# Context attention: output projections in 64x128 tiles over four PSUM banks, and context values of both batches in one go

## The chip, the cores and the metric

The kernel runs on one core of a Trainium2 chip. The metric is device time in microseconds, the median of several runs. Matrix products run on TensorE (PE in the profile; PEld is its weight loads), element-wise work on VectorE (DVE), ScalarE (ACT) and GpSimd (POOL), and most transfers are issued by SyncE (SP). Matrix products write to PSUM, which has eight banks of 128 partitions by 512 fp32 values.

## The reference

All data are fp32. Two batches of 1024 tokens with 256 features go through a transformer block: self attention, attention to a context of 154 tokens with 192 features, and a gated feed-forward layer, each behind a layer norm and with a residual. There are 16 heads of 64.

```python
def _attention(xq, xkv, wq, wk, wv, wo, bo):
    q = (xq @ wq).reshape(B, S, N_HEADS, D_HEAD)
    k = (xkv @ wk).reshape(B, T, N_HEADS, D_HEAD)
    v = (xkv @ wv).reshape(B, T, N_HEADS, D_HEAD)
    attn = softmax(einsum('bihd,bjhd->bhij', q, k) * D_HEAD ** -0.5)
    out = einsum('bhij,bjhd->bihd', attn, v).reshape(B, S, D_ATTN)
    return out @ wo + bo

h = _layernorm(x, ln1_g, ln1_b)
x = _attention(h, h, sa_wq, sa_wk, sa_wv, sa_wo, sa_bo) + x
h = _layernorm(x, ln2_g, ln2_b)
x = _attention(h, cond_emb, ca_wq, ca_wk, ca_wv, ca_wo, ca_bo) + x
h = _layernorm(x, ln3_g, ln3_b)
p = h @ ff_w1 + ff_b1
a, gate = p[..., :D_FF], p[..., D_FF:]
x = (a * gelu(gate)) @ ff_w2 + ff_b2 + x
```

## The kernel before

**Units and steps.** The 16 heads are taken as 8 pairs, so that each attention has 16 units: unit `ui` is batch `ui // 8`, head pair `ui % 8`. The program is one stream written out by hand (`tc.manual_schedule`): each engine runs its instructions in the order in which the code issues them. Self attention is the loop over `p` (8 steps a unit), context attention the loop over `c` (3 steps a unit, `ui, n = divmod(c, 3)`: three, three and two of a batch's eight token tiles of 128). The feed-forward layer follows.

**A step of context attention.** `cross_first(c)` issues the scores on TensorE (L999, tile `sc`) and the maxima on DVE (L1004). Then the copies that earlier products left in `stores` are issued, and `then` issues the exponentials on ACT (L1017, three or two for each of two heads). A function passed to `then` as `between` is issued between the two heads' exponentials. In the next step POOL divides by the sums (L1028), and two steps on DVE transposes the weights in 32x32 blocks (`cross_drain`, L1044). What else a step does depends on `n`:

- First step (`n == 0`): `cross_values(ui - 2)` multiplies the weights of the unit before last with its values (L1064, tile `poc`), in 32x64 tiles over four banks, the two `mm` and the two `sum` banks. DVE and ACT copy them out (L1075).
- Second step (`n == 1`): `cross_queries` makes the next unit's queries (L411, tile `pq_ca`) in 64x128 tiles on the two `mm` banks. ACT copies them out (L426) in the third step, behind the second step's exponentials and ahead of the third's.
- Third step (`n == 2`): an output piece (`out_piece`, L523, tile `py_ca` or `py_sa`), in even units the context values of one batch for two head pairs (`context_values`, L961, tile `pv_ca`), a norm's transposes where one is due (L323, tile `ph_ln`), and another output piece.

Units 1 and 15 also run output pieces in their second step: two each. Unit 1 runs one in its third step, and the fourth of that group runs in unit 2.

**Banks.** `mm_tile` and `sum_tile` each go round two banks (L70, L73); scores have the other four. A bank can be written again when the engine that read it last is done.

**Output pieces.** `out_piece` multiplies two token tiles with the output weights of two head pairs in 128x128 tiles: four `matmul` calls into one bank. An fp32 `matmul` stands as two rows in the trace, so a piece is eight rows. DVE adds a piece to `x` in one instruction of 512 columns (L530). A group of two head pairs has four pieces a batch; `cross_beside` queues a group at the first step of each odd unit from 3 on.

**Rounds.** Self attention's groups go through `out_rounds` (L536) instead: four token tiles at a time in 64x32 tiles, over the two `sum` banks (first pair of tiles) and the two `mm` banks (second pair). Both 64-row halves of TensorE work at once on the two banks of a pair; then they swap banks. `cross(pair, 0)` of both pairs is issued at once; before each pair's swapped half, a one-element copy by ACT (`seen`, L556) reads the bank and so separates the halves. Four adds of 256 columns follow on DVE (L562).

**Context values.** `context_values(b, pr)` multiplies a batch's first 128 context tokens with the value weights of two head pairs: 192 features in two 96-row matmuls, four rows. ACT copies the result (L968), SP writes it to DRAM (L969) and reads it back four times in another layout (L973). The last context tokens of all heads come from `context_ends`, whose result lies in `ends` until it has been sent to DRAM. Unit 0's values are made in self attention's step `SA - 2`, together with the keys of the last two head pairs (`context_keys`, L898, tile `pk`).

**Norms.** `norm_beside` queues a norm's statistics, normalisation and transposes in `side`; `run_work` takes one of them a step, and transposes only in a third step with an `mm` bank. The second batch's norm ahead of context attention is queued in unit 2 (its transposes run in units 3 to 6), the first batch's norm ahead of the feed-forward layer in unit 11 (transposes in units 12 to 15); their statistics (L266) run on DVE.

**SP's queue.** `load_ahead` issues self attention's loads and moves after each step's exchange of maxima and sums between partitions (L610).

Of the kernel before, what the change touches and what calls it, by code (L numbers as in the profile page):

```python
# [8 lines left out]
F32 = mybir.dt.float32  # L9
# [4 lines left out]
P = 128  # L14
# [4 lines left out]
def tile_transformer_block(ctx: ExitStack, tc: tile.TileContext, a: dict, out: bass.AP):  # L19
    nc = tc.nc  # L20
# [9 lines left out]
    NQ = 4  # L30
# [116 lines left out]
    def load_weights(kind, pr, what):  # L147
# [3 lines left out]
        elif kind == "sa" or what == "q":  # L151
            wsl[kind, pr, what] = load_slice(f"{kind}_w{what}", pr * P, P, HR)
        elif pr % 2 == 0:
            wsl[kind, pr, what] = load_slice(f"{kind}_w{what}", pr * P, VC, CC)
# [381 lines left out]
    def out_rounds(b, g, tiles):  # L536

        o = oT["sa", b, g]
        py = [bank(f"pr{b}_{g}_{t}") for bank, t in zip([sum_tile] * 2 + [mm_tile] * 2, tiles)]

        def cross(pair, swapped):
            for i in range(HP):
                for f in range(0, P, KB):
                    for r in (1, 0):
# [3 lines left out]
                            py[at][f:f + KB, :D], lhsT=o[own, i, t0:t0 + KB],  # L548
                            rhs=wo["sa", b, g][own, i, :],
# [9 lines left out]
        def add(at):  # L559
# [3 lines left out]
            added.add(("sa", b, g, t))  # L563

        for pair in range(2):
            cross(pair, 0)
        return [lambda pair=pair: second(pair) for pair in range(2)], [
            lambda at=at: add(at) for at in range(4)]

# [239 lines left out]
    held, kept, rounds = [], [], []  # L809

    def self_beside(ui):
# [15 lines left out]
        if ui >= HP and ui % HP == 0:  # L827
            ob, og = divmod(ui // HP - 1, NQ)
            for t0 in range(0, NG * 2, 2):
                rounds.append(  # L830
                    (ob, og, [t + e for t in out_order("sa")[t0:t0 + 2] for e in range(2)]))
# [3 lines left out]
    coming, ahead_ends = [], []  # L835
    to_dram = [(1, 3), (1, 6), (3, 3)]
    from_dram = [(NU - 1, n) for n in (0, 3, 5)]

    def load_ahead(p):
# [17 lines left out]
        if ahead_ends and (ui == 1 and n == SH + 1 or ui == 2 and n in (0, 1, SH)):  # L857
            ahead_ends.pop(0)()
        if (ui, n) in to_dram:
# [94 lines left out]
    def context_values(b, pr, bank=mm_tile):  # L954
# [3 lines left out]
        v = vs["ca", b, pr // 2] = pt_.tile([P, NB, VC], F32, tag="V", name=f"v_ca{b}_{pr}")  # L958
        pv = bank(f"pv_ca{b}_{pr}")
        for c in range(2):  # L960
            nc.tensor.matmul(  # L961
                pv[:, :VC], lhsT=ctxT[:, c, b * TP:b * TP + P],
                rhs=wsl["ca", pr, "v"][:, c, :], start=(c == 0), stop=(c == 1),
            )

        def store():
            own = one.tile([P, VC], F32, tag="own_v", name=f"own_v{b}_{pr}")
            nc.scalar.copy(own, pv[:, :VC])  # L968
            later.insert(0, lambda: nc.sync.dma_start(out=vd[b, pr][:P, :], in_=own))  # L969

            def back(a0):
                for a4 in range(a0, a0 + 2):
                    nc.sync.dma_start(  # L973
                        out=v[a4 * KB:(a4 + 1) * KB, :, :],
                        in_=vd[b, pr].rearrange("(n p) d -> p n d", p=KB))

# [620 lines left out]
```

## Time and profile before

| | |
|---|---|
| median of 3 runs | 1060.45 us (1059.89 to 1060.54) |
| the profiled execution | 1060.44 us, its span 1058.6 us |
| granted TensorE clock | 1.00 |
| busy: PE, PEld, DVE, ACT, POOL | 1047.1, 740.3, 880.7, 658.9, 769.9 us |
| context attention's scores | first at 687.57 us, last at 886.73 us |

Busy time is a share of the whole span. A row of a timeline gives start, length, engine, line, tile, tile shape on TensorE (rows x columns of the array) and how many instructions are merged; in brackets stands idle time before it and what ended it. The length of a merged TensorE line reaches to the end of its last matmul, which overlaps the next line's first, so that differences of starts tell what a group takes.

### The profile page before, as it was taken

Reading aid. Unit: us, or ns where it says so; the run is one execution under the profiler, and the core shown is the slowest. Engines: PE = TensorE matmul, PEld = TensorE weight load, DVE = VectorE, ACT = ScalarE, POOL = GpSimd, SP = SyncE. Lnnn points to the kernel's source line nnn. Section 1 sums busy time; section 2 is a strip of 40 time slices with the busy share of each in tenths; the row PEclk is TensorE's granted clock in tenths of the full one; section 3 lists DMA queues with packets and bytes.
Section 4 is the critical chain, followed back from the end, with each engine's and each line's share of the span. In section 5 each row is a group of like instructions: output and inputs, shape, how many; then the busy total and the mean of one; then the engine's idle time right before and its main releaser. Section 6 shows DMA issues by size and latency. Waiting matters only on the chain.

```text
span 1058.6 us, 51303 instructions
## 1 busy us (share of the span) xinstructions
PE 1047.1 (99%) x21700; PEld 740.3 (70%) x21700; DVE 880.7 (83%) x1313; ACT 658.9 (62%) x2147; POOL 769.9 (73%) x1620
## 2 busy tenths in 40 slices
PE   8999999999999999999999999999999999999998
PEld 6456965556576666665786676666676667889997
DVE  5799999999899999999999999968776777675654
ACT  5776767777776766766776777666666655243221
POOL 2677777788778777777777777757665777598773
PEclk9999999999999999999999999999999999999999
DMA  4322221121121021122122012135323221000000
GB/s 106 95 65 60 50 61 42 45 54 34 25 54 45 15 54 45 29 44 55 24 44 50 21 39 56 49 104 132 101 59 83 69 59 41 1 11 11 21 11 30
DMA packets 96023, 52.87 MB, mean 50 GB/s; under 512 B 30314, under 2 KB 93810, under 8 KB 95794
## 3 DMA queue, kind: packets, MB, share of 16 engines
q1 hardware_dynamic: 94466, 48.93, 18.9%
q8 instruction: 171, 2.80, 1.1%
q10 hardware_dynamic: 1328, 0.66, 0.2%
q14 instruction: 58, 0.48, 0.1%
HBM read 36.23 MB, written 4.39 MB: 38 GB/s over the span
## 4 chain that ended last, share of the span: by engine, by line
PE 90%; DVE 4%; ACT 2%; POOL 2%; issue 1%; DMA 1%; SPq 0%; DVEq 0%; POOLq 0%; ACTq 0%
PE s L583 20%; PE po L639 20%; PE pv_sa L443 5%; PE py_ca L523 5%; PE pk_sa L411 5%; PE pq_sa L411 5%; PE pr L547 5%; PE pf L1289 5%; PE poc L1064 4%; PE pb L1169 4%; PE pq_ca L411 4%; PE sc L999 3%; PE pa L1169 2%; PE pc L1169 2%; PE ph_ln L323 1%
## 5 line engine op out<-in xcount | busy, mean ns | idle before, releaser
L600 ACT ACTIVATE p<-s,st 128x512 f32<-128x512 f32 x512 | 345.4, 685 | 152.8 <-DVE st L592 121.4
L706 POOL TENSOR_SCALAR p<-p,rd,ee 128x512 f32<-128x512 f32 x508 | 385.2, 768 | 75.5 <-DVE rd L698 75.1
L592 DVE TENSOR_REDUCE st<-s 128x2 f32<-128x1024 f32 x256 | 308.7, 1207 | 49.9 <-issue 16.1
L733 DVE STREAM_TRANSPOSE pT<-p 128x1024 f32<-128x1024 f32 x256 | 303.9, 1221 | 2.4 <-POOL p L706 2.3
L583 PE MATMUL s<-k_sa,q_sa 64*32 64x512 f32 x4096 | 256.7, 590 | 1.1 <-DVE k_sa L432 0.6
L639 PE MATMUL po<-pT,v_sa 64*32 64x256 f32 x6144 | 180.5, 376 | 1.7 <-ACT p L1017 1.6
L639 PEld LDWEIGHTS po<-pT,v_sa 64*32 64x32 f32 x6144 | 142.7, 106 | 45.0 <-issue 15.2
L583 PEld LDWEIGHTS s<-k_sa,q_sa 64*32 64x32 f32 x4096 | 102.8, 106 | 78.5 <-issue 51.4
L1017 ACT ACTIVATE p<-sc,neg 128x154 f32<-128x154 f32 x256 | 97.1, 406 | 72.2 <-DVE rden L1025 70.2
L1028 POOL TENSOR_SCALAR p<-p,rden 128x154 f32<-128x154 f32 x256 | 96.8, 399 | 52.9 <-DVE rden L1025 51.9
L600 ACT ACTIVATION_READ_ACCUMULATOR p<-s,st 128x1 f32 x512 | 103.0, 201 | 0.0
L1004 DVE TENSOR_REDUCE neg<-sc 128x6 f32<-128x924 f32 (+1 forms) x48 | 48.1, 1003 | 20.2 <-PE sc L999 20.0
L523 PE MATMUL py_ca<-ca_wo,o_ca 128*128 128x256 f32 x256 | 61.1, 385 | 0.0
L639 PE MATMUL po<-pT,third_v 64*32 64x256 f32 x2048 | 60.5, 376 | 0.0
L443 PE MATMUL pv_sa<-sa_wv,home 64*32 64x256 f32 x2048 | 60.2, 376 | 0.0
L443 PEld LDWEIGHTS pv_sa<-sa_wv,home 64*32 64x32 f32 x2048 | 48.4, 106 | 14.1 <-issue 5.4
L411 PE MATMUL pq_sa<-home,sa_wq 64*32 64x512 f32 (+1 forms) x976 | 58.0, 586 | 0.0
L411 PE MATMUL pq_ca<-home,ca_wq 64*128 64x512 f32 (+1 forms) x352 | 57.8, 589 | 0.0
L639 PEld LDWEIGHTS po<-pT,third_v 64*32 64x32 f32 x2048 | 46.6, 106 | 16.0 <-issue 4.6
L1017 ACT ACTIVATION_READ_ACCUMULATOR p<-sc,neg 128x1 f32 x256 | 56.5, 221 | 0.0
L627 POOL TENSOR_TENSOR zz<-ee,st 128x8 f32<-128x8 f32 x128 | 25.8, 202 | 42.1 <-ACT ee L625 42.1
L411 PE MATMUL pk_sa<-home,sa_wk 64*32 64x512 f32 x960 | 56.3, 589 | 0.0
(144 smaller groups left out, 1576.1 us busy)
## 6 DMA issues: line engine op xcount, KB each, us to landing
st<-st SPq DMA_DIRECT2D x510, 1.0 KB, 1.7
v_sa<-v_sa SPq DMA_DIRECT2D x24, 256.0 KB, 3.3
v_ca<-vd SPq DMA_DIRECT2D x32, 160.0 KB, 3.4
sa_wq<-in_L_xattn_sa_wq_dram SPq DMA_DIRECT2D x32, 128.0 KB, 3.3
sa_wk<-in_L_xattn_sa_wk_dram SPq DMA_DIRECT2D x32, 128.0 KB, 3.1
sa_wv<-in_L_xattn_sa_wv_dram SPq DMA_DIRECT2D x32, 128.0 KB, 3.3
ca_wq<-in_L_xattn_ca_wq_dram SPq DMA_DIRECT2D x32, 128.0 KB, 3.0
wf<-in_L_xattn_ff_w_dram SPq DMA_DIRECT2D x12, 256.0 KB, 4.8
```

The lines of the kernel that those rows point to most:

```text
L411: nc.tensor.matmul(pq[r][f:f + m, at:at + n], lhsT=wt[own, c, f:f + m], rhs=h[own, c, t0:t0 + n], start=(c == 0), stop=(c == NH - 1), tile ...
L443: nc.tensor.matmul(pv[r][f:f + KB, i * VC:(i + 1) * VC], lhsT=h[own, c, t0:t0 + KB], rhs=wt[own, c, :], start=(c == 0), stop=(c == NH - 1) ...
L523: nc.tensor.matmul(py[:, e * D:(e + 1) * D], lhsT=o[:, i, (t + e) * P:(t + e + 1) * P], rhs=wo[kind, b, g][:, i, :], start=(i == 0), stop= ...
L583: nc.tensor.matmul(sc[a4 * KB:(a4 + 1) * KB, j, :], lhsT=q[r, c:c + KB], rhs=k[r, h * HB:(h + 1) * HB], start=True, stop=True, tile_positi ...
L592: nc.vector.tensor_reduce(st[:, 0, 0, i, :], sc, AX.X, ALU.max, negate=True)
L600: nc.scalar.activation(pr[:, j, :], sc[:, j, :], AF.Exp, bias=st[:, 0, 0, i, j:j + 1], accum_out=st[:, 0, 1, i, j:j + 1],)
L639: nc.tensor.matmul(po[a2][d:d + KB, :QH // 2], lhsT=v[r, t, e, d:d + KB], rhs=pT[r, d // DH * NK + n, :], start=(t == 0 and e == 0), stop= ...
L706: nc.gpsimd.tensor_scalar(pr[:, j, :], pr[:, j, :], v["rd"][:, c:c + 1], v["ee"][:, 0, c:c + 1], op0=ALU.mult, op1=ALU.mult,)
L733: nc.vector.transpose(halves[h][:, :, c:c + KB], slot[p]["members"][i].rearrange("p j (n k) -> p (j n) k", k=KB))
L1017: nc.scalar.activation(pr_[:, j, i, :T], sc[:, j, i * T:(i + 1) * T], AF.Exp, bias=neg[:, j, i:i + 1], accum_out=den[:, j, i:i + 1],)
L1028: nc.gpsimd.tensor_scalar(pr_[:, j, i, :T], pr_[:, j, i, :T], rden[:, j, i:i + 1], 1.0, op0=ALU.mult, op1=ALU.mult,)
L1169: nc.tensor.matmul(into[:, :BT], lhsT=lhs, rhs=wh[pair][i], start=first, stop=True, skip_group_check=True)
```

## The change

- `out_rounds` takes the kind of attention and a tile width `m`; `four_by_four` queues a group as two rounds. The last group of self attention and context attention's groups but the last are queued so. At a third step, and at the second step of units 1 and 15, one round is taken: with `m = 128` over four banks (64x128 tiles), its first halves right behind the scores, its swapped halves through `between` ahead of each head's exponentials, its adds at the start of the next step. Where a norm's transposes are due at a third step, the round becomes two pieces of `out_piece` as before.
- `then` takes a list of functions: with two, one ahead of each head's exponentials.
- `context_values(pr, bank)` makes the values of both batches: 192 features in three 64-row matmuls a batch, batch 0 on the array's upper and batch 1 on its lower 64 rows, on both `mm` banks, at the very end of units 2, 4 and 6 and in self attention for unit 0. Units 8, 10, 12 and 14 only read theirs back from DRAM.
- The context for this lies in the memory of `ends`, filled by eight small DMAs (`context_beside`) in units 3 to 6 of self attention. The value weights are loaded twice, once for each half of the partitions, and no longer for batch 1.

```diff
@@ -151,7 +151,11 @@
...
         elif pr % 2 == 0:
-            wsl[kind, pr, what] = load_slice(f"{kind}_w{what}", pr * P, VC, CC)
+            t = wsl[kind, pr, what] = wpool.tile(
+                [P, DC // HR, VC], F32, tag="wv", name=f"{kind}_w{what}_{pr}")
+            own = w[f"{kind}_w{what}"][:, pr * P:pr * P + VC].rearrange("(c p) f -> p c f", p=HR)
+            for r0 in range(0, P, HR):
+                nc.sync.dma_start(out=t[r0:r0 + HR], in_=own)
...
@@ -533,20 +537,20 @@
...
-    def out_rounds(b, g, tiles):
-        o = oT["sa", b, g]
+    def out_rounds(kind, b, g, tiles, m=KB):
+        o = oT[kind, b, g]
         py = [bank(f"pr{b}_{g}_{t}") for bank, t in zip([sum_tile] * 2 + [mm_tile] * 2, tiles)]
...
             for i in range(HP):
-                for f in range(0, P, KB):
+                for f in range(0, P, m):
                     for r in (1, 0):
...
                         nc.tensor.matmul(
-                            py[at][f:f + KB, :D], lhsT=o[own, i, t0:t0 + KB],
-                            rhs=wo["sa", b, g][own, i, :],
+                            py[at][f:f + m, :D], lhsT=o[own, i, t0:t0 + m],
+                            rhs=wo[kind, b, g][own, i, :],
                             start=swapped == 0 and i == 0, stop=swapped == 1 and i == HP - 1,
...
@@ -560,12 +564,20 @@
...
             nc.vector.tensor_tensor(xs, py[at][:, :D], xs, ALU.add)
-            added.add(("sa", b, g, t))
+            added.add((kind, b, g, t))
...
+    rounds = []
+    def four_by_four(kind, b, g):
+        pairs = out_order(kind)
+        for i in range(0, len(pairs), 2):
+            rounds.append((kind, b, g, [t + e for t in pairs[i:i + 2] for e in range(2)]))
...
@@ -806,7 +818,7 @@
...
-    held, kept, rounds = [], [], []
+    held, kept = [], []
...
@@ -826,13 +838,12 @@
...
             ob, og = divmod(ui // HP - 1, NQ)
-            for t0 in range(0, NG * 2, 2):
-                rounds.append(
-                    (ob, og, [t + e for t in out_order("sa")[t0:t0 + 2] for e in range(2)]))
+            four_by_four("sa", ob, og)
         if ui in (4, 6):
...
     coming, ahead_ends = [], []
+    both = []
     to_dram = [(1, 3), (1, 6), (3, 3)]
...
@@ -856,6 +867,8 @@
...
             ahead_ends.pop(0)()
+        if both and ui > SH - 2 and n in ((SH + 1, SH + 2) if ui % 2 else (0, 1)):
+            both.pop(0)()
         if (ui, n) in to_dram:
...
@@ -951,31 +964,63 @@
...
-    def context_values(b, pr, bank=mm_tile):
...
-        v = vs["ca", b, pr // 2] = pt_.tile([P, NB, VC], F32, tag="V", name=f"v_ca{b}_{pr}")
-        pv = bank(f"pv_ca{b}_{pr}")
-        for c in range(2):
-            nc.tensor.matmul(
-                pv[:, :VC], lhsT=ctxT[:, c, b * TP:b * TP + P],
-                rhs=wsl["ca", pr, "v"][:, c, :], start=(c == 0), stop=(c == 1),
-            )
+    both_ctx = ends[:, :DC // HR * P].rearrange("p (c k) -> p c k", k=P)
+    def context_beside():
...
+        moves = []
+        for b in range(B):
+            for c in range(DC // HR):
+                f = c * HR
+                while f < (c + 1) * HR:
+                    half, row = divmod(f, CC)
+                    n = min((c + 1) * HR - f, CC - row)
+                    to = b * HR + f - c * HR
+                    moves.append(lambda b=b, c=c, half=half, row=row, n=n, to=to: nc.sync.dma_start(
+                        out=both_ctx[to:to + n, c, :],
+                        in_=ctxT[row:row + n, half, b * TP:b * TP + P]))
+                    f += n
+        return moves
+    def hold_values(b, pr):
+        v = vs["ca", b, pr // 2] = pt_.tile([P, NB + B, VC], F32, tag="V", name=f"v_ca{b}_{pr}")
+        return v
+    def spread_values(b, pr, at):
+        def back(a0):
+            for a4 in range(a0, a0 + 2):
+                nc.sync.dma_start(
+                    out=vs["ca", b, pr // 2][a4 * KB:(a4 + 1) * KB, :NB, :],
+                    in_=vd[b, pr].rearrange("(n p) d -> p n d", p=KB))
+        later.insert(at, lambda: back(0))
+        later.insert(at + 1, lambda: back(2))
+    def context_values(pr, bank):
...
+        v = hold_values(0, pr)
+        pv = [bank(f"pv_ca{b}_{pr}") for b in range(B)]
+        for c in range(DC // HR):
+            for b in range(B):
+                own = slice(b * HR, (b + 1) * HR)
+                nc.tensor.matmul(
+                    pv[b][:, :VC], lhsT=both_ctx[own, c, :], rhs=wsl["ca", pr, "v"][own, c, :],
+                    start=(c == 0), stop=(c == DC // HR - 1), tile_position=(b * HR, 0))
+        def out(b):
+            nc.sync.dma_start(out=vd[b, pr][:P, :], in_=v[:, NB + b, :])
         def store():
-            own = one.tile([P, VC], F32, tag="own_v", name=f"own_v{b}_{pr}")
-            nc.scalar.copy(own, pv[:, :VC])
-            later.insert(0, lambda: nc.sync.dma_start(out=vd[b, pr][:P, :], in_=own))
-            def back(a0):
-                for a4 in range(a0, a0 + 2):
-                    nc.sync.dma_start(
-                        out=v[a4 * KB:(a4 + 1) * KB, :, :],
-                        in_=vd[b, pr].rearrange("(n p) d -> p n d", p=KB))
-            later.insert(2, lambda: back(0))
-            later.insert(3, lambda: back(2))
+            for b in range(B):
+                nc.scalar.copy(v[:, NB + b, :], pv[b][:, :VC])
+            later.insert(0, lambda: [out(b) for b in range(B)])
+            spread_values(0, pr, 2)
...
@@ -1006,13 +1051,13 @@
...
-        def then(between=None):
+        def then(between=()):
             pr_ = pp_.tile([P, 2, TG, NB * KB], F32, tag="P", name=f"p_{c}")
...
             for j in range(2):
-                if j and between:
-                    between()
+                for fn in between[j:j + 1] if len(between) > 1 else between if j else ():
+                    fn()
                 for i in range(nt):
...
@@ -1081,7 +1126,7 @@
...
         if ui > HP and ui % HP == 1:
-            out_pieces("ca", *divmod(ui // HP - 1, NQ), out_order("ca"))
+            four_by_four("ca", *divmod(ui // HP - 1, NQ))
         if ui == NU - 5:
...
@@ -1377,6 +1422,7 @@
...
         side.append((True, (), turn_rows))
+        both.extend(context_beside())
         work.append(costing(2, lambda: self_queries(*units[0], P, 2 * P)))
...
@@ -1417,7 +1463,7 @@
...
                     hold_late_keys()
-                    run(lambda: context_values(*units[0]))
+                    run(lambda: context_values(0, mm_tile))
                     for pr in range(NKD, NPAIR):
...
@@ -1433,21 +1479,23 @@
...
             if c == SH:
-                out_pieces("sa", B - 1, NQ - 1, out_order("sa"))
+                four_by_four("sa", B - 1, NQ - 1)
                 w1, w2, parts = hold_gated()
...
             ui, n = divmod(c, len(CG))
+            b = units[ui][0]
             nxt = units[ui + 1] if ui + 1 < NU else None
...
             elif n == 2 and nxt and ui:
-                load_weights("ca", nxt[1], "v")
+                if not nxt[0]:
+                    load_weights("ca", nxt[1], "v")
             flush(adds)
-            between = None
+            between, taken = (), ()
             if c < 2:
...
@@ -1459,14 +1507,22 @@
...
                     slot[SA - 1]["dd"] = differences(SA - 1, slot[SA - 1]["st"])
-                    between = lambda: softmax_join(SA - 1)
+                    between = [lambda: softmax_join(SA - 1)]
             flush(stores)
...
             if n == 0 and ui > 1:
-                own, between = cross_values(ui - 2, [mm_tile] * 2 + [sum_tile] * 2)
-                lates.append(then(between))
+                banks = [mm_tile] * 2 + [sum_tile] * 2
+                own, copy = cross_values(ui - 2, banks)
+                lates.append(then([copy]))
                 own()
             else:
+                beside = n == 2 and side and side[0][0] and added.issuperset(side[0][1])
+                if rounds and (n == 2 or n == 1 and (ui == 1 or not nxt)):
+                    if beside:
+                        kind, ob, og, tiles = rounds.pop(0)
+                        out_pieces(kind, ob, og, tiles[::2])
+                    else:
+                        between, taken = out_rounds(*rounds.pop(0), P)
                 lates.append(then(between))
...
@@ -1483,22 +1539,23 @@
...
                 spare["turned"] = True
-                if ui == 1 or not nxt:
-                    run_work(2, 0)
-                else:
+                if ui > 1 and nxt:
                     run(lambda: cross_queries(*nxt))
...
                 flush(adds)
-                if ui and ui % 2 == 0:
-                    run(lambda: context_values(*units[ui]))
                 run_work(0, 1, mm_tile)
                 flush(stores)
-                if ui > 1:
-                    run_work(0, 0, n_sum=1)
+                run_work(0, 0, n_sum=1)
+                if ui and ui % 2 == 0 and not b:
+                    run(lambda: context_values(ui, mm_tile))
+                elif b and ui % 2 == 0:
+                    hold_values(*units[ui])
+                    spread_values(*units[ui], 0)
                 if ui and ui % HP == 0:
                     load_out("ca", *divmod(ui // HP - 1, NQ))
+            adds.extend(taken)
             if c == 0:
...
```

## Prediction

> **What bounds the kernel now.** I read the page's totals and chain first, then PE's, ACT's and DVE's timelines of single units of context attention.
>
> ```profile
> span 1058.6 us, 51303 instructions
> PE 1047.1 (99%) x21700; PEld 740.3 (70%) x21700; DVE 880.7 (83%) x1313; ACT 658.9 (62%) x2147; POOL 769.9 (73%) x1620
> PE 90%; DVE 4%; ACT 2%; POOL 2%; issue 1%; DMA 1%; SPq 0%; DVEq 0%; POOLq 0%; ACTq 0%
> ```
>
> TensorE is busy 99% of the span and holds 90% of the chain. So the change is priced in TensorE time: rows issued, plus holes opened. The profiled execution took 1060.44 us (span 1058.6), 0.01 us from the median 1060.45 of the runs, so a sum made on it carries over. About 0.2% (2.1 us) is what a measurement can tell from no change.
>
> The end of unit 9 on PE (start, length, rows). The last matmul of a line overlaps the next line, so I take differences of starts:
>
> ```profile
> 805.57 1.06 PE L999 MATMUL sc<-third_v,q_ca 64*128 64x154 f32 x12
> 806.46 3.60 PE L411 MATMUL pq_ca<-home,ca_wq 64*128 64x512 f32 x16
> 809.89 0.69 PE L999 MATMUL sc<-third_v,q_ca 64*128 64x154 f32 x8
> 810.51 3.72 PE L523 MATMUL py_ca<-ca_wo,o_ca 128*128 128x256 f32 x16
> 814.16 1.06 PE L999 MATMUL sc<-third_v,q_ca 64*128 64x154 f32 x12
> 815.15 0.47 PE L1064 MATMUL poc<-pT_ca,v_ca 32*64 32x256 f32 x8
> ...
> 824.27 1.03 PE L961 MATMUL pv_ca<-ca_wv,ctxT 96*128 96x256 f32 x4
> 825.13 1.89 PE L523 MATMUL py_ca<-ca_wo,o_ca 128*128 128x256 f32 x8
> ...
> 715.30 2.41 PE L1064 MATMUL poc<-pT_ca,v_ca 32*64 32x256 f32 x80
> 717.64 1.06 PE L999 MATMUL sc<-third_v,q_ca 64*128 64x154 f32 x12
> ...
> 19.59 2.00 PE L411 MATMUL pq_sa<-home,sa_wq 64*128 64x256 f32 x16
> ```
>
> No line shows a wait. The reader is to see the cost of changing the tile shape. Twelve score rows take 0.89 us when entered from 32x64 tiles and followed by queries in their own shape (805.57 to 806.46). Before `py_ca` the eight score rows take 0.62, and `py_ca` takes 3.65 for 16 rows, where context values inside the same shape run at 0.86 for 4 rows (824.27 to 825.13), 3.44 for 16: 0.21 for its entry and exit. I take 0.10 for each entry and each exit.
>
> **Part 1: outputs in 64x128 tiles, the work itself.** Sixteen 64x128 rows of 512 columns take 3.43 us (806.46 to 809.89), so the 32 rows of 256 columns of a four-tile round take the same 3.43, in four quarters of 0.86; the 19.59 line, the one group in exactly that form, agrees: 16 rows are over 2.00 us after the first start, a shape change and the last row's tail included, so 64x128 rows of 256 columns do overlap in pairs. That is no less than the 3.44 of two 128x128 pieces. Only the shape changes go: 0.62 + 3.65 + 0.99 (the scores of 814.16, entered and left across a change) = 5.26 becomes 0.52 + 3.43 + 0.89 = 4.84, a gain of 0.42 a round.
>
> The Trainium skill's page "TensorEngine Tiling (Array Packing)", section Tiling Modes, says that changing the mode drains TensorE. The trace agrees, with about 0.1 us on each side; by that rule alone the sum would be the first rival's.
>
> **Part 1: what a round waits for.** The old pieces used only the two sum banks in a unit's third step. A round also takes both mm banks, and these hold the next unit's queries until ACT has copied them out. ACT of unit 9, then four rows of unit 4 (PE, PE, ACT, DVE):
>
> ```profile
> 808.67 0.39 ACT L1017 ACTIVATE p<-sc,neg 128x154 f32<-128x154 f32 x1 [1.19 <-DVE rden L1025]
> ...
> 810.87 1.11 ACT L426 ACTIVATE q_ca<-pq_ca 128x512 f32<-128x512 f32 x2
> 811.83 0.43 ACT L1017 ACTIVATE p<-sc,neg 128x154 f32<-128x154 f32 x1
> ...
> 748.71 1.13 PE L961 MATMUL pv_ca<-ca_wv,ctxT 96*128 96x256 f32 x4 [0.16 <-ACT q_ca L426]
> 749.67 0.60 PE L323 MATMUL ph_ln<-ident,xn_ln 128*128 128x128 f32 x4
> ...
> 748.03 0.62 ACT L426 ACTIVATE q_ca<-pq_ca 128x512 f32<-128x512 f32 x1
> ...
> 750.32 1.37 DVE L334 TENSOR_SCALAR home<-ph_ln,cols 128x128 f32<-128x128 f32 x4
> ```
>
> Six exponentials (808.67 to 810.87, 0.37 each) stand ahead of the copies, which end at 811.98. The round's first quarter, on the sum banks, ends at 809.89 + 0.52 + 0.86 = 811.27. The second quarter's first matmul takes the bank of the second copy, and everything on PE is queued behind it: the other quarters, the next scores and value products. Unit 4 shows the form of such a wait: its matmul starts at 748.71, 0.06 after the first copy ends (748.03 + 0.62), and its four rows then take 0.96 instead of 0.86. So the second quarter waits from 811.27 to 812.04 and loses 0.10 more: 0.87. A round costs 0.87 - 0.42 = +0.45. The cover that hid the copies was the 128x128 piece on the sum banks.
>
> Behind that, ACT's small copy between halves and the adds:
>
> ```profile
> L556 ACT COPY seen<-pr x28: 132/132/133, 135.0 to 660.4; 1x1 f32<-1x1 f32 x28
> L562 DVE TENSOR_TENSOR x<-pr,x x56: 382/388/425, 136.6 to 672.6; 128x256 f32<-128x256 f32 x56
> ```
>
> The first `seen` follows the query copies at 811.98 and is done long before the third quarter (812.9); the second comes two exponentials later (0.73), ahead of the fourth (813.7). I cost them at nothing here. Of the four adds the last two follow the round's end by 0.1 and take under 0.8, while the next scores cover 0.89: nothing either, 0.3 a round if DVE is late.
>
> The Trainium skill's page "TensorEngine Tiling (Array Packing)", section Restrictions and Gotchas (Gotcha 1: PSUM Pressure), says that row tiles write to different banks and so raise the pressure on PSUM. That speaks against this change; of the trace of before, the 0.16 us idle in the line at 748.71 are of this kind.
>
> **The units one by one.** Rounds replace pieces in units 1, 7 to 11 and the second step of 15; units 3 to 6 and 12 to 15 have a norm's transpose at the third step and keep 128x128 pieces there.
>
> Units 7 and 9: +0.45 each. Units 8 and 10 also lose their context values (0.86): -0.41 each. Unit 11, where the third norm's statistics delay DVE and so ACT:
>
> ```profile
> 834.61 0.69 PE L999 MATMUL sc<-third_v,q_ca 64*128 64x154 f32 x8
> 839.86 3.02 PE L1064 MATMUL poc<-pT_ca,v_ca 32*64 32x256 f32 x80
> ...
> 836.64 1.11 ACT L426 ACTIVATE q_ca<-pq_ca 128x512 f32<-128x512 f32 x2
> ```
>
> Its first quarter ends at 835.99, the copies at 837.75: 1.82 + 0.10 waited, less 0.42, less the 0.61 that the following value products waste today (3.02 against 2.41) and that the later start hides: +0.89. Units 12 and 14 lose context values, nothing else: -0.86 each. Units 7 to 14: 0.90 - 0.82 + 0.89 - 1.72 = -0.75.
>
> Unit 15 runs a round in its second step, where mm is free. There the second `seen` is behind three exponentials, and those behind DVE's maxima:
>
> ```profile
> 882.09 1.06 PE L999 MATMUL sc<-k,q_ca 64*128 64x154 f32 x12
> 887.45 1.99 PE L523 MATMUL py_ca<-ca_wo,o_ca 128*128 128x256 f32 x8
> ...
> 885.23 0.39 ACT L1017 ACTIVATE p<-sc,neg 128x154 f32<-128x154 f32 x1 [1.24 <-DVE rden L1025]
> ```
>
> Three quarters end at 882.09 + 0.89 + 2.58 = 885.56; `seen` ends at 885.23 + 1.10 + 0.13 = 886.46. The last quarter starts at 886.52 and ends, with the 0.10, at 887.48; scores 0.62 end at 888.10 against 887.45: +0.65.
>
> Units 1 and 2:
>
> ```profile
> 707.03 1.06 PE L999 MATMUL sc<-third_v,q_ca 64*128 64x154 f32 x12
> 721.97 0.69 PE L999 MATMUL sc<-third_v,q_ca 64*128 64x154 f32 x8
> 726.72 2.59 PE L1064 MATMUL poc<-pT_ca,v_ca 32*64 32x256 f32 x80
> ...
> 709.35 0.39 ACT L1017 ACTIVATE p<-sc,neg 128x154 f32<-128x154 f32 x1 [1.56 <-DVE rden L1025]
> ...
> 724.00 1.11 ACT L426 ACTIVATE q_ca<-pq_ca 128x512 f32<-128x512 f32 x2
> ```
>
> Unit 1 now finishes the self outputs in two rounds, of which today one piece runs in unit 2. First round: three quarters end at 707.03 + 0.89 + 2.58 = 710.50, `seen` at 709.35 + 1.10 + 0.13 + 0.06 = 710.64, the round at 711.60; then 0.52 + 3.43 + 0.89 puts the value products at 716.44 instead of 715.30: +1.14. In unit 2 that piece no longer covers the copies. Both values banks are free at 725.11; the two batches' 12 rows take 12 x 0.107 = 1.29, so value products start near 725.17 + 1.29 + 0.10 + 0.89 = 727.45, not 726.72, and no longer waste 0.18 (2.59 against 2.41): +0.55.
>
> **Part 2: context values.** Both batches take 1.29 where one took 0.86: +0.43 in units 4 and 6, with no more shape changes. In unit 4 one of the two banks is the transposes' own. DVE frees it around 751.5 (the 1.37 us line, moved to the end of the add before it), while PE would be there at 751.1 (the transposes now start at 748.71): 0.4 more, 0.83 in all. Unit 0's values are made in the last unit of self attention:
>
> ```profile
> 679.02 1.13 PE L961 MATMUL pv_ca<-ca_wv,ctxT 96*128 96x256 f32 x4
> 679.99 2.32 PE L898 MATMUL pk<-ctxT,ca_wk 96*128 96x320 f32 x8
> 683.49 1.23 DVE L592 TENSOR_REDUCE st<-s 128x2 f32<-128x1024 f32 x1 [0.39 <-ACT k L902]
> ```
>
> 1.29 + three changes of 0.10 instead of 0.97: +0.62. DVE's maxima sat idle 0.39 for what precedes them, so the delay goes on into the chain; bounds 0 and 0.62, and I take 0.62.
>
> **Queues.** SP issues eight more small copies in units 3 to 6 of self attention, after a step's exchange, at about the 0.58 of
>
> ```profile
> L162 SPq DMA_DIRECT2D x<-in_x_dram x8: 580/580/582, 68.1 to 197.2; - x8
> ```
>
> which sit in such steps now. A step lasts some 5 us and they have no reader until unit 0's values, so 0; 1 us if SP's exchange slipped each time by a tenth. Two loads replace one per weight slice, but batch 1's are gone: 0.
>
> **Sum:** 0.62 + 1.14 + 0.55 + 0.83 + 0.43 - 0.75 + 0.65 = +3.47 on 1060.44, so 1063.9 us, 0.33% slower.
>
> **Rivals.** (1) The waits do not come, because the banks are free in time. Then six rounds (7 to 11 and 15) gain 0.42 each, 2.5; units 8, 10, 12 and 14 give up 3.4; units 1 and 2 gain 1.3 instead of losing 1.7 (716.19 instead of 716.44, and in unit 2 0.52 + 1.29 + 0.89 in place of 726.72 - 721.97 + 0.18); units 0, 4 and 6 pay 0.62 + 0.86. That is -5.8: 1054.6 us, faster. It decides where the copies end before 811.27; the ACT line at 810.87 speaks against it. 7%. (2) The rounds in 7 to 11 wait half as long, because ACT gets to its copies sooner: 1.8 + 0.9 less, +0.8, 1061.2, no change. ACT's 1.19 of idle time ahead of line 808.67 is for it; that its end is set by DVE, whose order the change leaves alone there, is against. 15%. (3) The adds or a `seen` come late in each of the eight rounds as well, 0.4 each: +6.7, 1067.1. DVE's 83% is for it; that it is free at 812.63, ahead of the adds, is against:
>
> ```profile
> 811.44 1.19 DVE L1044 STREAM_TRANSPOSE pT_ca<-p 128x480 f32<-128x480 f32 x2
> ```
>
> 12%. That the pairs of 64 rows do not overlap at all would add 3.4 a round; the 19.59 line excludes it. The forecast: 66%.
>
> **How the numbers follow.** Slower takes the forecast and (3), less a little at its lower end: 0.77. Same takes (2) and that end: 0.16. Faster is (1): 0.07. The range leaves out (1) and half of (3): it runs from (2) with unit 0's delay absorbed (0.6 less), 1060.5, to 1066.5.
>
> **What would show it.** Right: in units 7 to 11 a hole on PE after the first eight output rows, ended by ACT L426, of 0.8 us and in unit 11 of 1.8; before unit 2's values a hole of 2.6; in unit 15 one of 1.0 ended by `seen`; no shape change around rounds, with scores of 0.52 before them; 64x128 value rows gone from units 8 to 14. Wrong: rounds of 3.43 without a hole (then rival 1), or idle time of `poc` behind DVE's adds (rival 3).

## The result, and the profile after

| | before | after |
|---|---|---|
| median on the same chip | 1060.49 us (1059.89 to 1062.07, 6 runs) | 1065.55 us (1063.52 to 1067.44, 6 runs) |
| profiled execution, its span | 1060.44 us, 1058.6 us | 1065.62 us, 1063.8 us |
| granted clock in the profile | 1.000 | 0.998 |

The changed kernel is slower: ratio 1.0046, 95% interval 1.0034 to 1.0059. The forecast was 1063.9 us in a range of 1060.5 to 1066.5, so sign, range and most of the mechanism held; the size is 1.65 us short, and one term is to blame.

The page's totals and the shares of its chain, after:

```profile
span 1063.8 us, 51635 instructions
PE 1049.2 (99%) x21844; PEld 733.5 (69%) x21844; DVE 881.7 (83%) x1329; ACT 660.7 (62%) x2163; POOL 773.5 (73%) x1620
PE 86%; DVE 5%; ACT 3%; POOL 2%; issue 2%; DMA 2%; SPq 1%; DVEq 0%; POOLq 0%; ACTq 0%
```

PE's busy time grew by 2.1 us, the span by 5.2. The rest is idle PE, which the view of PE's waits names for context attention (waited for, total us, times, longest):

```profile
PE pv_ca L1012 <- ACT q_ca L430: 1.8, 1, 1.8
PE pr L551 <- ACT q_ca L430: 1.1, 1, 1.1
PE pr L551 <- ACT seen L560: 0.7, 1, 0.7
PE ph_ln L327 <- ACT q_ca L430: 0.5, 2, 0.3
```

The first is unit 2's values, the second unit 11's round, the third unit 15's. PE's timeline of unit 9, and ACT's copies in it (start, length):

```profile
815.37 0.69 PE L1044 MATMUL sc<-third_v,q_ca 64*128 64x154 f32 x8
815.89 4.24 PE L551 MATMUL pr<-ca_wo,o_ca 64*128 64x256 f32 x31
...
821.06 2.41 PE L1109 MATMUL poc<-pT_ca,v_ca 32*64 32x256 f32 x80
...
816.33 1.11 ACT L430 ACTIVATE q_ca<-pq_ca 128x512 f32<-128x512 f32 x2
817.28 0.16 ACT L560 COPY seen<-pr 1x1 f32<-1x1 f32 x1
```

Scores to value products take 821.06 - 815.37 = 5.69 us; before it was 815.15 - 809.89 = 5.26. That is +0.43 where +0.45 was forecast. The first quarter ends at 815.89 + 0.86 = 816.75 and the copies at 817.44, so the second quarter stands for 0.7 us inside a group that the timeline draws as one line: a wait of this length between rows of one line shows in no bracket, only in the difference of starts.

Unit 11, unit 15 and unit 2 in the same view:

```profile
840.08 0.69 PE L1044 MATMUL sc<-third_v,q_ca 64*128 64x154 f32 x8
840.60 1.03 PE L551 MATMUL pr<-ca_wo,o_ca 64*128 64x256 f32 x8
842.76 3.13 PE L551 MATMUL pr<-ca_wo,o_ca 64*128 64x256 f32 x23 [1.13 <-ACT q_ca L430]
...
846.81 2.41 PE L1109 MATMUL poc<-pT_ca,v_ca 32*64 32x256 f32 x80
...
886.69 1.06 PE L1044 MATMUL sc<-k,q_ca 64*128 64x154 f32 x12
887.58 2.85 PE L551 MATMUL pr<-ca_wo,o_ca 64*128 64x256 f32 x24
891.12 1.13 PE L551 MATMUL pr<-ca_wo,o_ca 64*128 64x256 f32 x8 [0.69 <-ACT seen L560]
...
892.71 1.99 PE L527 MATMUL py_ca<-ca_wo,o_ca 128*128 128x256 f32 x8
...
724.12 0.69 PE L1044 MATMUL sc<-third_v,q_ca 64*128 64x154 f32 x8
726.62 2.98 PE L1012 MATMUL pv_ca<-ca_wv,ends 64*128 64x256 f32 x11 [1.81 <-ACT q_ca L430]
...
731.06 2.20 PE L1109 MATMUL poc<-pT_ca,v_ca 32*64 32x256 f32 x72
```

Unit 11 takes 6.73 from scores to value products against 5.25 before, unit 15 takes 6.02 from scores to the next piece against 5.36: +1.48 (0.61 of it given back in unit 12) and +0.66, as forecast. In unit 2 the hole is there, and what follows it is strange: twelve value rows and twelve score rows take 731.06 - 726.62 = 4.44 us, though the forecast gave 2.28 for them. The windows view says why (window, length, busy us of PE, PEld, DVE, ACT and POOL, then the granted clock, the DMA share and GB/s):

```profile
724.00:727.10 3.10, 1.29 (x12) 0.75 (x8) 3.03 (x10) 3.10 (x15) 2.95 (x9) 1.00 0.00 0
727.10:730.60 3.50, 3.50 (x21) 3.15 (x21) 1.40 (x6) 2.18 (x10) 3.34 (x10) 0.51 0.04 12
730.60:734.00 3.40, 3.40 (x93) 2.62 (x93) 1.72 (x4) 1.59 (x8) 3.22 (x7) 1.00 0.61 171
```

Behind the hole TensorE was granted half its clock for some 3.5 us, and then the whole again.

Unit by unit, as differences between the starts of each unit's value products, after less before (unit 3 gives back 0.18 of unit 2's 2.37, so the two stand together):

| unit | 0 | 1 | 2 and 3 | 4 | 6 | 7 | 8 | 9 | 10 | 11 and 12 | 14 | 15 | sum |
|---|---|---|---|---|---|---|---|---|---|---|---|---|---|
| forecast | 0.62 | 1.14 | 0.55 | 0.83 | 0.43 | 0.45 | -0.41 | 0.45 | -0.41 | 0.03 | -0.86 | 0.65 | 3.47 |
| measured | 0.63 | 1.20 | 2.19 | 0.93 | 0.43 | 0.44 | -0.49 | 0.44 | -0.44 | 0.01 | -0.87 | 0.66 | 5.13 |

Self attention ends 0.14 us later in this execution, and the end gives 0.06 back: the span's 5.2. In the profiles of the eight kernels beside before this start differs by 0.14 to 1.93 us, for no reason that their edits give, so these differences, which leave it out, are sharper than the times.

### The profile page after: what moved, and what is told of

The parts are those of the page before. It is cut to its first block, busy times and chain, and to the rows that moved or that the text cites. A ratio compares the mean times of both kernels' runs of the same rounds, so it can differ in the third digit from the quotient of the medians.

```text
span 1063.8 us, 51635 instructions
## 1 busy us (share of the span) xinstructions
PE 1049.2 (99%) x21844; PEld 733.5 (69%) x21844; DVE 881.7 (83%) x1329; ACT 660.7 (62%) x2163; POOL 773.5 (73%) x1620
## 4 chain that ended last, share of the span: by engine, by line
PE 86%; DVE 5%; ACT 3%; POOL 2%; issue 2%; DMA 2%; SPq 1%; DVEq 0%; POOLq 0%; ACTq 0%
PE po L651 20%; PE s L595 19%; PE pr L551 7%; PE pv_sa L447 5%; PE pk_sa L415 5%; PE pf L1334 4%; PE pq_sa L415 4%; PE pb L1214 4%; PE poc L1109 4%; PE py_ca L527 3%; PE sc L1044 2%; PE pq_ca L415 2%; PE pa L1214 2%; PE pc L1214 2%; ACT p L1062 2%
## 5 line engine op out<-in xcount | busy, mean ns | idle before, releaser
L651 PEld LDWEIGHTS po<-pT,v_sa 64*32 64x32 f32 x6144 | 138.8, 106 | 48.5 <-issue 16.2
L595 PEld LDWEIGHTS s<-k_sa,q_sa 64*32 64x32 f32 x4096 | 100.5, 106 | 81.5 <-issue 52.5
L551 PE MATMUL pr<-sa_wo,o_sa 64*32 64x256 f32 (+1 forms) x1856 | 59.8, 377 | 0.0
L551 PEld LDWEIGHTS pr<-sa_wo,o_sa 64*32 64x32 f32 (+1 forms) x1856 | 46.7, 109 | 15.1 <-issue 5.5
```

The costliest lines, as they stand in the source:

```text
L551: nc.tensor.matmul(py[at][f:f + m, :D], lhsT=o[own, i, t0:t0 + m], rhs=wo[kind, b, g][own, i, :], start=swapped == 0 and i == 0, stop=swap ...
L595: nc.tensor.matmul(sc[a4 * KB:(a4 + 1) * KB, j, :], lhsT=q[r, c:c + KB], rhs=k[r, h * HB:(h + 1) * HB], start=True, stop=True, tile_positi ...
L651: nc.tensor.matmul(po[a2][d:d + KB, :QH // 2], lhsT=v[r, t, e, d:d + KB], rhs=pT[r, d // DH * NK + n, :], start=(t == 0 and e == 0), stop= ...
```

## Experiments

Theory A: every term but one is as forecast (a round loses more to the wait for the query copies than the shape changes bring), and unit 2's excess is clock lost behind the hole. The rivals were that the values' new form, both halves of the array at once, is slow by itself, and that the rounds lose their time to something other than the two banks. All ratios are to the kernel before, run again on the same chip (median 1061.98 us over 23 runs for e1 to e4, 1061.96 over 21 for h1, g1 and g2; in the table above it took 1060.49, so times are to be compared by these ratios).

**Filling the hole (e1).** The changed kernel, with eight idle products in unit 2 ahead of the values; nobody reads them.

```diff
+                if ui == 2:
+                    fill = [sum_tile(f"fill{r}") for r in range(2)]
+                    for i in range(4):
+                        for r in range(2):
...
+                            nc.tensor.matmul(
+                                fill[r][:, :VC], lhsT=both_ctx[own, 0, :], rhs=wsl["ca", ui, "v"][own, 0, :],
...
                 if ui and ui % 2 == 0 and not b:
                     run(lambda: context_values(ui, mm_tile))
```

> Eight matmuls in 64x128 tiles on the two sum banks, whose result nobody reads, stand in unit 2 between the scores of the third step and the context values; all else is the changed kernel. They take 8 x 2 rows x 0.107 = 1.7 us of the 2.0 us in which TensorE waited there for the query copies, so they add nothing by themselves. Theory A (the idle time made the clock gate cut TensorE's clock to 0.61 for the next 4.4 us): the granted clock stays at 1.00, the 12 value rows take 1.4 us as in unit 6 instead of 2.8, the 12 score rows 0.9, and the kernel takes 1.6 to 2.1 us less than the changed one: 1063.5 to 1064.0, ratio to before about 1.003. Rival B (the value rows and scores were slow for another reason, as a transfer at the same time): they stay slow, 1065.5, ratio 1.0047.

Measured: 1065.26 us (1064.93 to 1066.36, 6 runs), ratio 1.0033 (1.0021 to 1.0045), clock 1.0 in all six executions. PE's timeline of unit 2:

```profile
725.53 0.69 PE L1044 MATMUL sc<-third_v,q_ca 64*128 64x154 f32 x8
726.06 1.89 PE L1556 MATMUL fill<-ca_wv,ends 64*128 64x256 f32 x16
728.03 1.83 PE L1012 MATMUL pv_ca<-ca_wv,ends 64*128 64x256 f32 x11
...
730.80 2.41 PE L1109 MATMUL poc<-pT_ca,v_ca 32*64 32x256 f32 x80
```

From scores to value products it takes 730.80 - 725.53 = 5.27 us, with more work in it, where the changed kernel took 731.06 - 724.12 = 6.94. The same values in the same form lose nothing here, so their form is not to blame. The two ratios' intervals overlap; it is the trace and the clock that carry this, not the time. With the clock kept, the steps from unit 0 on come to +3.40 us, against the forecast's +3.47.

**The `seen` copies first (e4).** The changed kernel, with both separating copies ahead of the exponentials in second steps.

```diff
                         between, taken = out_rounds(*rounds.pop(0), P)
+                        if n == 1:
+                            between = [lambda two=between: [fn() for fn in two], lambda: None]
```

> The changed kernel with one edit: in second steps (units 1 and 15) both small copies between a round's halves are issued ahead of all the exponentials instead of one ahead of each head's. Theory A (unit 15's round waits 1.0 us because its second copy stands behind three exponentials): that hole and unit 1's 0.2 go, as the exponentials there wait for DVE's maxima anyway: 1.2 to 1.3 us less than the changed kernel, 1064.3, ratio about 1.0035. Rival B (the last quarter waits for its bank): no change, 1065.5, ratio 1.0047.

Measured: 1064.66 us (1062.8 to 1066.88, 11 runs), ratio 1.0026 (1.0017 to 1.0035). Unit 15 comes to -0.31 instead of +0.66 and unit 1 to +0.96 instead of +1.20, as theory A had it: the last quarter there waited for `seen`. No wait is left in unit 15's round, which takes 890.25 - 886.70 = 3.55 us:

```profile
886.70 3.72 PE L551 MATMUL pr<-ca_wo,o_ca 64*128 64x256 f32 x32
890.25 0.69 PE L1044 MATMUL sc<-k,q_ca 64*128 64x154 f32 x8
```

This kernel still has unit 2's hole, and its profile, taken in an execution that kept the clock, shows that hole without the loss:

```profile
724.93 0.69 PE L1044 MATMUL sc<-third_v,q_ca 64*128 64x154 f32 x8
727.44 1.83 PE L1012 MATMUL pv_ca<-ca_wv,ends 64*128 64x256 f32 x11 [1.82 <-ACT q_ca L430]
...
730.20 2.41 PE L1109 MATMUL poc<-pT_ca,v_ca 32*64 32x256 f32 x80
```

The hole is as long (1.82 against 1.81), the rows behind it take 730.20 - 727.44 = 2.76 instead of 4.44, and the whole again takes 5.27: with the clock kept, units 2 and 3 cost 0.69 - 0.18 = +0.51, and the forecast was +0.55. So the loss comes in some executions only: 5 of 11 at a mean clock of 0.998, with a mean of 1065.8 us, and the other six at 0.999 or 1.0, with a mean of 1063.8. Of the changed kernel's own six, four were at 0.998 (mean 1066.1) and two at 1.0 (mean 1064.5).

**The hole in the kernel before (h1).** The values in their old form, the last self piece moved from unit 2 to unit 1.

```diff
-                if ui > 1:
+                if ui > 0:
                     run_work(0, 0, n_sum=1)
```

> The kernel before, with the last self piece moved from unit 2's third step into unit 1's, so that unit 2's values, in their old form of four rows of 96x128, stand right behind the scores and wait for the query copies. It asks whether the hole by itself costs the clock. Theory A (an idle PE of about 2 us can lower the granted clock for some 3 us): unit 1 +1.72, unit 2 a hole on PE of 2.0 to 2.2 us ended by ACT L426, and about -0.2 instead of the piece's -1.9: +1.5 us with the clock kept, 1062.0 on the time before; in part of the executions, say a third to two thirds, the clock falls to 0.5 behind the hole as in the changed kernel, and these take 1.6 to 2 us more, 1063.8. Rival (the clock was lost to the values' new form, both halves of the array at once): no execution below 1.0, all at +1.5.

Measured: 1064.25 us (1061.66 to 1066.8, 9 runs), ratio 1.0023 (1.0012 to 1.0035). Four executions at 0.998 (1064.25, 1065.66, 1065.84 and 1066.8 us, mean 1065.6), five at 1.0 (1061.66 to 1064.25, mean 1063.2). The profiled one kept its clock:

```profile
723.94 0.69 PE L999 MATMUL sc<-third_v,q_ca 64*128 64x154 f32 x8
726.64 1.13 PE L961 MATMUL pv_ca<-ca_wv,ctxT 96*128 96x256 f32 x4 [2.01 <-ACT q_ca L426]
...
728.68 2.59 PE L1064 MATMUL poc<-pT_ca,v_ca 32*64 32x256 f32 x80
```

Here is a hole of 2.01 us in front of four old rows, and four executions of nine have the lower mean clock. Where in these four it fell, no trace shows; 3.5 us at 0.51 in a span of some 1064 would give a mean of 0.998, and none of the 44 executions of the kernel before whose clock is known, without this hole, was below 0.999. So the hole does it, without rounds and without the new values. The times of the two sorts touch: 1064.25 us stands in both. The move alone costs 1.72 us (unit 1 gets the piece, unit 2 saves nothing by its absence: the copies set the end either way).

**Pieces everywhere (e2).** The changed kernel with 128x128 pieces wherever it has rounds, in the places where they were before; the values of both batches stay.

```diff
-                beside = n == 2 and side and side[0][0] and added.issuperset(side[0][1])
+                beside = True
...
-                run_work(0, 0, n_sum=1)
+                if ui > 1:
+                    run_work(0, 0, n_sum=1)
```

> The changed kernel with all output projections of context attention (and the last group of self attention) in 128x128 pieces at the places of the kernel before; only the context values of both batches at a unit's end are left of the change. Theory A (the rounds' waits cost what the sum says, and the unit 2 hole comes from the piece that left it): unit 0 +0.6, unit 2 +0.6 (its piece covers all but 0.8 us of the wait, too short to lose the clock), unit 4 +0.9, unit 6 +0.4, units 8, 10, 12 and 14 -0.86 each, self attention +0.1: -0.8 in all, 1059.7, ratio 0.9992, granted clock 1.00. Rival B (the values are the costly part): 1063 or more, ratio over 1.002.

Measured: 1060.71 us (1059.39 to 1061.96, 11 runs), ratio 0.9986 (0.9977 to 0.9995). Its steps are +0.63 in unit 0, +0.02 in unit 1, +0.53 in unit 2, +0.91 and +0.43 in units 4 and 6, 0.0 in 7, 9, 11 and 15, and -0.87, -0.87, -0.86 and -0.87 in 8, 10, 12 and 14: -0.95 us together. The context values are a small gain. The loss lies in what this run takes out together: the rounds, and the self piece that they moved out of unit 2, which in h1 cost 1.72 us and, in some executions, the clock.

**Query copies on DVE (e3).** The changed kernel, with DVE in place of ACT copying the queries, right behind them.

```diff
...
+            for r in (1, 0):
+                nc.vector.tensor_scalar(
+                    q[:, r * S // 2:(r + 1) * S // 2], pq[r], scale, 1.0, op0=ALU.mult, op1=ALU.mult)
...
                 if ui > 1 and nxt:
                     run(lambda: cross_queries(*nxt))
+                    flush(stores)
```

> The changed kernel with one edit: VectorE instead of ScalarE copies the context queries out of their two banks, issued right behind the queries instead of behind the next scores, the bank first that a round asks for first. Theory A (the rounds of units 7 to 11 wait for the query copies' banks): DVE is free 3.9 us after a unit's value products and the queries end at 4.3, so the banks are free at about 5.2 and 5.8 while the second quarter starts at 5.7; the holes of 0.8 in units 7 to 10 and 1.8 in unit 11 go to 0.2 or less, the hole in unit 2 from 2.0 to about 1.4, units 4 and 13 lose their 0.4. That is -3 -1.6 -0.6 -0.7, and 1.6 to 2.1 more if the shorter hole in unit 2 keeps the clock: 1057.5 to 1060, ratio 0.997 to 0.9995. Rival B (the rounds wait for the small copy between the halves, or ACT's and DVE's order is only shifted): holes of the same length, ended by `seen`, and 1065 or more, ratio over 1.004.

Measured: 1065.42 us (1064.14 to 1065.8, 6 runs), ratio 1.003 (1.0019 to 1.0042). A miss: I had expected it to beat the kernel before. The same stretch as unit 9 above, and what PE waited for:

```profile
814.39 0.69 PE L1050 MATMUL sc<-third_v,q_ca 64*128 64x154 f32 x8
814.91 3.89 PE L551 MATMUL pr<-ca_wo,o_ca 64*128 64x256 f32 x32
818.59 1.00 PE L1050 MATMUL sc<-third_v,q_ca 64*128 64x154 f32 x12
819.52 2.56 PE L1115 MATMUL poc<-pT_ca,v_ca 32*64 32x256 f32 x80
...
814.61 1.29 DVE L902 TENSOR_SCALAR q_ca<-pq_ca 128x512 f32<-128x512 f32 x2 [0.82 <-PE pq_ca L415]
...
PE pr L551 <- ACT seen L560: 1.4, 2, 0.7
PE poc L1115 <- ACT v_ca L1027: 1.4, 1, 1.4
PE poc L1115 <- DVE x L566: 0.7, 1, 0.7
```

Unit 9 falls from 5.69 to 819.52 - 814.39 = 5.13 us, below the 5.26 of before: the wait for the copies was the round's loss. But the round, 3.68 us, is not down to its rows' 3.43 (the copies still end at 815.90, 0.13 after the first quarter's 815.77; the rest is open), and new waits stand where ACT or DVE now come late: in unit 2 the copies of the values (1.4), in units 11 and 15 a `seen`, in unit 11 the adds. By the steps, units 7 to 10 win 1.76 us, and units 2, 6, 11 to 14 lose 1.6 again against the changed kernel with its clock kept (0.78 of it in unit 6: there DVE frees the transposes' bank at 781.51, while PE comes to the values at 780.95, and their rows lag as in unit 4; in the changed kernel it was free at 781.65, ahead of 781.75). Theory A's cause holds; my price for this cure did not.

**Versions meant to beat both (g1, g2).** Pieces at every third step; one round in unit 1's second step and one in unit 15's, with both `seen` first; of the other two self pieces one in unit 1's third step and one ahead of unit 2's values (g2), or both ahead of unit 2's values (g1); the first batch's values on a sum bank. The main lines that both have:

```diff
-                beside = n == 2 and side and side[0][0] and added.issuperset(side[0][1])
+                beside = n == 2
...
+                        between = [lambda two=between: [fn() for fn in two], lambda: None]
...
-                    run(lambda: context_values(ui, mm_tile))
+                    run(lambda: context_values(ui, [sum_tile, mm_tile]))
```

> The changed kernel with its uncovered waits taken out: pieces of 128x128 tiles at every third step; one round in unit 1's second step and one in unit 15's, both `seen` copies ahead of the exponentials; the other two self pieces both in unit 2's third step, ahead of the values, whose first batch goes to a sum bank. Theory A (a round loses more to the bank wait than the shape changes bring, and the values need a piece in front of them): unit 0 +0.63; unit 1 -2.54 and unit 2 +1.55 (a piece moved from one to the other, 1.72, the rest -0.99); unit 4 and unit 6 +0.43 each; units 8, 10, 12 and 14 -0.86 each; unit 15 -0.31: -3.3 us against the kernel before, ratio 0.997, and the clock at 1.0 in every execution. Rival (what the pieces saved in e2 was the most there is: scores of unit 1's last step, now right behind the round, wait for ACT or DVE instead): unit 1 no less than -1.7 and the whole near -2.4, 0.998; or a hole there of 1.6 us or more, with no gain left in units 1 and 2 at all, -1.7.

Measured: 1060.6 us (1059.65 to 1063.47, 11 runs), ratio 0.9987 (0.9978 to 0.9995). By the steps it is -1.8 us, not theory A's -3.3. The rival's wait is there, but of 0.25 us and not of 1.6: unit 1 gives -1.99 and units 2 and 3 +2.50, because the scores behind the round wait 0.25 us for ACT's exponentials, the scores ahead of the pieces take 0.4 longer, which I did not trace to a cause, and unit 3's transposes now wait for query copies (0.24):

```profile
713.93 0.70 PE L1044 MATMUL sc<-third_v,q_ca 64*128 64x154 f32 x8
714.88 1.06 PE L1044 MATMUL sc<-third_v,q_ca 64*128 64x154 f32 x12 [0.25 <-ACT p L1062]
...
739.05 0.63 PE L327 MATMUL ph_ln<-ident,xn_ln 128*128 128x128 f32 x4 [0.24 <-ACT q_ca L430]
```

> As g1, but one of the two self pieces stays in unit 1's third step, so that unit 2 has one piece ahead of its values, as in the kernel before. Theory A: the wait for the query copies is in part uncovered in unit 2 (+0.71 -0.18 as in e2), unit 1 -0.24, unit 0 +0.63, unit 4 +0.43 to +0.9, unit 6 +0.43, units 8, 10, 12 and 14 -0.86 each, unit 15 -0.31: -1.6 to -2.0 us, ratio 0.998, clock 1.0. Rival (one piece in front is enough for the values when one of their banks is a sum bank): unit 2 near 0, -2.4 us.

Measured: 1059.64 us (1058.23 to 1061.35, 7 runs), ratio 0.9979 (0.9968 to 0.999), clock 1.0 in all: faster than the kernel before by 2.3 us. Here the rival is right: one piece is cover enough, since the values begin on the free sum bank behind it:

```profile
723.32 1.99 PE L527 MATMUL py_sa<-sa_wo,o_sa 128*128 128x256 f32 x8
725.24 1.69 PE L1012 MATMUL pv_ca<-ca_wv,ends 64*128 64x256 f32 x12
...
881.35 3.72 PE L551 MATMUL pr<-ca_wo,o_ca 64*128 64x256 f32 x32
884.90 0.69 PE L1044 MATMUL sc<-k,q_ca 64*128 64x154 f32 x8
```

Unit 2 costs 0.24, unit 4 0.44 instead of 0.93, unit 1 gains 0.39 and unit 15 0.30: from unit 0 on -2.43 us. Without its waits a round takes 884.90 - 881.35 = 3.55 us, or 3.46 in unit 1, close to the 3.43 that the forecast gave for the rows alone.

## Why the prediction was right, and where it was short

- **Rounds in 64x128 tiles (+0.45 each).** Right, 0.43 to 0.44 in units 7 and 9: both the 3.43 us of rows and the wait for the bank of the second copy are shown, the first by the last experiment's 3.46, the second by the copies moved to DVE, though they brought only 0.56 of the 0.87 us that the forecast gave for the wait. The hole of 0.8 that was to be seen on PE is there, but hidden within a line.
- **Units 11 and 15.** Right, 0.01 for 11 and 12 together against 0.03, and 0.66 against 0.65; that `seen` is unit 15's wait is shown by issuing it first (-0.97).
- **Context values.** Unit 0's 0.63 came out in full, as taken; 0.43 in unit 6 and -0.86 to -0.87 in units 12 and 14 also. Unit 4 was +0.93 for +0.83; the 0.4 forecast for the transposes' bank stands in the rows as 0.49 (units 4 and 6 of the changed kernel):

```profile
755.24 1.83 PE L1012 MATMUL pv_ca<-ca_wv,ends 64*128 64x256 f32 x11
...
756.97 1.11 PE L1044 MATMUL sc<-third_v,q_ca 64*128 64x154 f32 x10
758.01 2.41 PE L1109 MATMUL poc<-pT_ca,v_ca 32*64 32x256 f32 x80
...
781.75 1.57 PE L1012 MATMUL pv_ca<-ca_wv,ends 64*128 64x256 f32 x12
783.14 0.95 PE L1044 MATMUL sc<-k,q_ca 64*128 64x154 f32 x12
784.03 2.42 PE L1109 MATMUL poc<-pT_ca,v_ca 32*64 32x256 f32 x80
```

From values to value products it is 2.77 us in unit 4 and 2.28 in unit 6, without a hole that a bracket shows: one batch's rows start and the other's lag. In g2, where the values no longer take that bank, unit 4 costs 0.44.
- **Unit 1.** +1.20 for +1.14.
- **Unit 2, the term that was mis-sized: +0.55 forecast, +2.19 measured.** With the clock kept the term comes to +0.51 or +0.52 (e4 and e1), but in part by luck. The wait itself was priced too high: the values begin behind the first copy and not the second, so the hole is 1.8 us and not 2.6; their rows and the scores then take 2.76 and not 2.28, and scores to value products comes to +0.52 where the sum had +0.73. What makes up for it is 0.18 that the sum had not: the value products at unit 2's start take longer behind unit 1's round (2.60 against 2.41). The part of the size that failed is what the hole costs. I priced the hole at its own length and not at what it does to the clock: 1.68 us more (4.44 against 2.76 for the same rows). That is about the distance between 1063.9 and 1065.55. The trace of before gave no warning; its one long hole in this part of the kernel kept the clock (none of 44 executions below 0.999):

```profile
698.81 3.69 PE L639 MATMUL po<-pT,v_sa 64*32 64x256 f32 x128 [1.63 <-ACT p L1017]
```

- **Rivals.** The first needed the copies done in time; they were not. The second's half wait did not come. The third's late adds appear only where DVE got more to do. The total came out between the forecast and the third rival, by a mechanism that was in neither.

## What to carry to other kernels

A product that is moved into the place of a covering piece starts when the copies behind its banks end, so price it from that row, and look for a bank that is free earlier: a sum bank for one batch brought back 0.5 us in unit 4. A tile shape that saves 0.4 us of shape changes but needs two more banks is worth it only where these banks are idle, as in unit 15, where it brought 0.3 once `seen` came first. And a hole of about 2 us on a busy TensorE is to be priced twice, by its length and by the chance that the clock falls behind it.

## What the runs showed of the hardware

- Behind idle time of 1.8 us on PE the granted clock fell to half for some 3.5 us (0.51 over 727.10 to 730.60); that is seen in one trace. The mean clock of 0.998 that goes with it stands in 13 of 26 executions of the three kernels that have a hole of 1.8 to 2.0 us in unit 2 (4 of 6, 5 of 11 and 4 of 9). It cost 1.68 us in the trace, and between executions of the same kernel 1.6, 1.9 and 2.4 us in the means. The five kernels in which that hole is filled, covered or shortened (e1, e2, e3, g1, g2; in e3 one of 1.36 us stands there in its place) showed no execution below 0.999, nor did the kernel before, which has its 1.63 us hole in another place. The Trainium skill's page "TensorE: Matmul & The Clock Gate", section "Why this matters for your kernels", asks for no idle gaps over about 3 us and names one idle window as the condition; here 1.8 us, in a stretch where PE was busy 1.29 of 3.10 us, was enough. The same page of the Trainium skill, section "What's actually happening", says that the window runs freely, about 3.4 us long; that would fit a loss that comes by chance and lasts 3.5 us, but no run here shows the window itself. Whether 1.63 us is safe by its length or only by its place was not tried.
- Products on the two 64-row halves lost part of their overlap where they did not run in step: the twelve value rows take 783.14 - 781.75 = 1.39 us in unit 6, and 756.97 - 755.24 = 1.73 in unit 4, where one half starts later than the other.
